# Rotated keys from a permutation of raw keys, and free-engine choice for standardisation and addends, in a planned three-layer decoder kernel

## The chip, the cores and the metric

The kernel runs on one core of a Trainium2 chip. A core has five engines with queues of their own: TensorE (PE, matmuls and transposes; PEld is its loading of the stationary operand), VectorE (DVE), ScalarE (ACT), GpSimd (POOL), and SyncE (SP), which here issues all DMAs. The metric is the device time of one execution in microseconds, and the times given are medians over several runs of the same program.

## The reference, cut to what matters

Two sequences (batches) of 512 tokens with 1024 features pass through three layers, each with a residual: an attention with 32 heads and 8 key heads and sign weights; a "state" layer; and a dense layer with low-rank additions. In float32 throughout. The change lies in the state layer's attention (16 heads of 16), in normalisations, and in how softmax maxima are handed to the scores.

```python
def rope(x, pos):                       # half = 8
    ang = pos[..., None] * inv
    cos, sin = jnp.cos(ang)[:, :, None, :], jnp.sin(ang)[:, :, None, :]
    x1, x2 = x[..., :half], x[..., half:]
    return jnp.concatenate([x1 * cos - x2 * sin, x2 * cos + x1 * sin], axis=-1)
...
qkv_in = rat_read(layernorm(x), read_w, read_g, read_b, 3)   # grouped read, then normalised to 256 x 3
q, k, v = (y @ w.T for y, w in zip(split(qkv_in, 3), qkv_w))
q, k = rope(q, pos), rope(k, pos)
p = softmax(where(causal, q @ k.T / sqrt(16), -1e30))
o = p @ v
```

After it come a write of `o` back into the state (`rat_write`), a second read of two parts, a gated unit over 1024 context columns, and a second write.

## The kernel before

The whole program is one sequence of named steps, written as Python generators (`build`, L1656 on). Each `yield` names an engine, a cost in us and the time at which its inputs are ready. A small planner (`run`) takes at each turn the step that can start first, plus its lag, and emits its instructions; the lags of jobs stand in `build`, those of spawned sub-jobs in the table `LAGS`. What the planner emits is pinned in that order, so the order on each engine is fixed when the program is built. On the chip each engine runs its own queue in order and waits on semaphores, whatever costs the planner assumed.

Buffers come from pools with fixed counts: 2 PSUM `bank`s (128x512 f32), 3 PSUM `pair`s (two banks each), and `slab`, `probs`, `page`, `row` tiles in SBUF. A step that needs a buffer takes one that an earlier step has given back.

The jobs, for batches 0 and 1:

- `in0`, `in1`, `k`, `v`, `q`, `wo`, `proj0`, `proj1`: inputs split into three bf16 parts, sign weights, projections of the first attention.
- `maxA`, `maxB` (`peaks_1`): row maxima of the scores of the first attention, 8 groups of 4 heads per batch. TensorE makes scores into two pairs, DVE reduces each pair (`reduced`). When a group of four query tiles is done, `turned` splits the negated maxima (128x16) into three bf16 addends in `parts` with four DVE operations; TensorE transposes them into a bank (`maxB_bank`), and ACT copies them to a `shift` tile.
- `attA`, `attB` (`attend`): scores again, transposed, plus a matmul of a 3x128 block of `ones16` with `shift`, which adds the negated maximum; ACT takes the exponentials; DVE adds them up; TensorE multiplies them with the values.
- `outA`, `outB`: output projection, with clean-up on DVE and POOL; rows are stored to `kept`.
- `rot`, `tableA`, `tableB`: sines and cosines and their layout into a table of 3 x 512 columns: for queries, for keys, for keys with halves exchanged.
- `stateW`, `stateA`, `stateB` (`state_inputs`): load a row, statistics, standardise 128x1024 on DVE, then `read`: transposes, a grouped matmul, statistics of three parts of 256, standardise each on DVE, transpose back with gains. Then projections: three weights `proj[0..2]` with four groups each. Each group takes two matmuls of 128x512 in f32 into a bank. Queries (kind 0) are multiplied by their table into `qq`; keys (kind 1) into `kk`; kind 2 is the key weight with the halves of each head exchanged, multiplied by the third table into a row and added to `kk` (`rotated`).
- `maxC`, `attC`, `maxD`, `attD`: the same two passes as above for the state attention, causal, four groups each. maxC works on stateA's result, maxD on stateB's.
- `tailW`, `tailA`, `tailB` (`tail`): write, second `read` with two parts of 256, gated unit, second write.
- `factor`, `factorsB`, `weights`, `denseA`, `denseB`: low-rank factors and the dense layer.

The third key weight and its use, as they stand before:

```python
for kind in range(3):
    t = yield from self.fetch(self.proj[kind], a["proj"][:, kind], 512)
...
for kind, (y, dst) in enumerate(((ys[0], qq), (ys[1], kk), (ys[1], None))):
    w = self.proj[kind]
```

In the profile all vector, scalar and GpSimd operations of the planned part have line L51 (a recording helper), all matmuls L130 and all transposes L133, so the tiles' names tell them apart: job, kind of buffer.

## Time and profile before

| what | us |
|---|---|
| median of 3 runs (1135.48 to 1136.71) | 1136.23 |
| the profiled execution | 1135.51 |
| its span on the core | 1133.8 |
| mean granted TensorE clock in it | 0.965 of full speed |

The profile's page gives for each engine its busy time, and a granted clock of TensorE in tenths per slice; a chain of waits that ended last, followed back from the last instruction; and groups of instructions by tile. A window view gives the busy time of every engine between two times. A view on one tile gives the instructions that write or read it, with the least, median and greatest duration in ns.

Where TensorE waited longest for another engine, in total, one instruction's waits together:

| TensorE instruction waits for | us | times | longest |
|---|---|---|---|
| transposes of the first input, for DVE | 8.7 | 1 | 8.7 |
| maxD scores, for DVE's maxima (buffers) | 3.9 | 5 | 2.2 |
| maxB transposes, for the addends on DVE | 3.4 | 1 | 3.4 |
| first dense transposes, for DVE | 3.2 | 2 | 2.8 |
| maxB scores, for DVE's maxima (buffers) | 3.1 | 7 | 0.9 |

### The profile page before, as it was taken

To read this page: it belongs to the slowest core of one execution; us is meant where nothing else is said; L and a number is where in the kernel's file an instruction comes from. 1 tells how busy PE (TensorE), PEld (TensorE's weight loads), DVE (VectorE), ACT (ScalarE), POOL (GpSimd) and SP (SyncE) were. 2 spreads that over 40 slices of the span, in tenths; PEclk is the share of its full clock that TensorE was granted. 3 is DMA by queue.
4 is the path that set the end of the run, shared out by engine and by line. 5 is a ranking of instruction groups with operands and counts; after the bars stand their busy time and mean duration, and the time that the engine had idled before them with its cause. 6 is when DMAs were issued, how large, how long until landed. Compare 5 with 4: busy or idle time off the path is not lost.

```text
span 1133.8 us, 16121 instructions
## 1 busy us (share of the span) xinstructions
PE 1063.1 (94%) x6364; PEld 521.5 (46%) x6364; DVE 841.2 (74%) x1390; ACT 442.8 (39%) x711; POOL 239.2 (21%) x249
## 2 busy tenths in 40 slices
PE   4889999999999998999999899989988899999998
PEld 3554353333233632332555543545465465665643
DVE  7978888578878865887777961599668677788572
ACT  6762101388500215786221255224743232332310
POOL 3442333322222303454451012001200000000000
PEclk9999999999998997999999889979998999999999
DMA  6621000101214221240113000410151001011110
GB/s 256 203 82 28 20 10 20 29 20 29 61 33 177 95 64 39 61 168 1 38 56 116 8 11 16 172 38 1 57 197 68 33 20 55 11 48 38 38 37 38
DMA packets 24784, 70.51 MB, mean 62 GB/s; under 512 B 5234, under 2 KB 5252, under 8 KB 23684
## 3 DMA queue, kind: packets, MB, share of 16 engines
q1 hardware_dynamic: 24708, 69.48, 17.9%
q8 instruction: 50, 0.82, 0.3%
q14 instruction: 26, 0.21, 0.1%
HBM read 50.59 MB, written 10.49 MB: 54 GB/s over the span
## 4 chain that ended last, share of the span: by engine, by line
PE 79%; DVE 11%; ACT 5%; issue 2%; DMA 1%; POOL 1%; SPq 0%; ACTq 0%; DVEq 0%; POOLq 0%
PE proj_bank L130 8%; PE denseA_pair L130 6%; PE denseB_pair L130 6%; PE attA_pair L130 4%; PE outA_bank L130 4%; PE attB_pair L130 4%; PE tailB_bank L130 3%; PE attB_bank L130 3%; PE attA_bank L130 3%; PE maxB_pair L130 3%; PE maxA_pair L130 3%; PE tailA_bank L130 3%; PE outB_bank L130 3%; PE stateB_bank L130 3%; PE tailB_pair L130 3%; PE tailA_pair L130 3%
## 5 line engine op out<-in xcount | busy, mean ns | idle before, releaser
L51 DVE TENSOR_REDUCE maxB_mx<-maxB_pair 128x2 f32<-128x1024 f32 x64 | 75.3, 1217 | 21.7 <-PE maxB_pair L130 21.3
L51 DVE TENSOR_REDUCE maxA_mx<-maxA_pair 128x2 f32<-128x1024 f32 x64 | 75.5, 1216 | 14.0 <-PE maxA_pair L130 14.0
L130 PEld LDWEIGHTS <-start_slab 128*128 128x128 bf16 x480 | 44.7, 98 | 68.8 <-issue 21.1
L51 DVE TENSOR_TENSOR attB_probs<-attB_probs,attB_probs 128x1024 f32<-128x1024 f32 x46 | 62.6, 1401 | 13.8 <-PE attB_bank L130 13.5
L51 ACT ACTIVATE attB_probs<-attB_pair 128x1024 f32<-128x1024 f32 x64 | 62.6, 1023 | 20.9 <-PE attB_pair L130 10.8
L51 DVE TENSOR_TENSOR attA_probs<-attA_probs,attA_probs 128x1024 f32<-128x1024 f32 x46 | 56.6, 1282 | 16.9 <-PE attA_bank L130 8.5
L51 ACT ACTIVATE attA_probs<-attA_pair 128x1024 f32<-128x1024 f32 x64 | 62.1, 1021 | 9.7 <-PE attA_pair L130 9.4
L130 PE MATMUL proj_bank<-in_slab,start_slab 128*128 128x512 bf16 x240 | 55.5, 379 | 1.7 <-ACT in_slab L51 1.7
L130 PE MATMUL proj_bank<-in_probs,start_slab 128*128 128x512 bf16 x240 | 54.7, 380 | 0.0
L130 PE MATMUL maxB_pair<-maxB_row,proj_slab 32*128 32x512 f32 x256 | 47.4, 687 | 3.1 <-DVE maxB_mx L51 3.1
L51 POOL TENSOR_SCALAR proj_row<-proj_row 128x512 f32<-128x512 f32 x24 | 47.7, 1987 | 1.9
L130 PE MATMUL outA_bank<-wo_slab,attA_slab 128*128 128x512 bf16 x192 | 46.7, 392 | 0.7 <-ACT maxB_shift L51 0.7
L130 PE MATMUL attB_pair<-proj_slab,attB_row 32*128 32x512 f32 x256 | 46.7, 685 | 0.0
L51 ACT ACTIVATE proj_row<-proj_bank,cs 128x512 f32<-128x512 f32 x20 | 13.7, 686 | 80.8 <-PE proj_bank L130 60.2
L130 PE MATMUL outB_bank<-wo_slab,attB_slab 128*128 128x512 bf16 x192 | 43.3, 379 | 0.3 <-POOL attB_slab L51 0.3
L130 PE MATMUL attA_pair<-proj_slab,attA_row 32*128 32x512 f32 x256 | 41.6, 639 | 0.3 <-ACT attA_probs L51 0.3
L51 POOL MEMSET tailB_row<- 9x128 f32 x8 | 1.6, 195 | 186.4 <-PE tailB_bank L133 70.7
L130 PE MATMUL attB_bank<-attB_probs,proj_slab 128*32 128x512 f32 x256 | 38.4, 633 | 1.1 <-DVE tableA_slab L51 0.7
L51 ACT COPY maxB_shift<-maxB_bank 128x512 bf16<-128x512 bf16 x8 | 4.7, 586 | 84.7 <-PE maxB_bank L133 84.7
L51 POOL TENSOR_SCALAR proj_slab<-proj_row 128x512 f32<-128x512 f32 x24 | 14.9, 621 | 106.6 <-ACT proj_row L51 89.0
L130 PE MATMUL maxA_pair<-maxA_row,proj_slab 32*128 32x512 f32 x256 | 36.8, 640 | 0.0
L51 POOL TENSOR_SCALAR_AFFINE_SELECT attD_probs<-attD_probs 128x512 f32<-128x512 f32 x16 | 12.1, 754 | 113.8 <-ACT attD_probs L51 104.3
(410 smaller groups left out, 2321.8 us busy)
## 6 DMA issues: line engine op xcount, KB each, us to landing
in_page<-in_x_dram SPq DMA_DIRECT2D x8, 512.0 KB, 4.1
q_page<-in_q_weight_dram SPq DMA_DIRECT2D x8, 512.0 KB, 5.3
wo_page<-in_o_weight_dram SPq DMA_DIRECT2D x8, 512.0 KB, 3.4
tailW_slab<-in_write_dram SPq DMA_DIRECT2D x3, 752.0 KB, 7.1
maxA_row<-proj_slab SPq DMA_DIRECT2D x32, 64.0 KB, 2.0
attA_row<-proj_slab SPq DMA_DIRECT2D x32, 64.0 KB, 2.0
maxB_row<-proj_slab SPq DMA_DIRECT2D x32, 64.0 KB, 2.0
outA_page<-in_x_dram SPq DMA_DIRECT2D x4, 512.0 KB, 3.7
```

The source lines that it names most:

```text
L51: return self.kernel.pin(getattr(self.engine, name)(*args, **kw))
L130: self.pin(self.nc.tensor.matmul(*args, **kw))
```

## The change

Five things are changed.

1. The third key weight is gone from the inputs, from the loads and from the projections. Keys are projected once into a bank. ACT copies the raw keys to a row, DVE multiplies the bank by the second table into `kk`, TensorE multiplies a constant 128x128 matrix `swap` (the identity with the halves of every 16 rows exchanged) with the raw row into a second bank, and DVE multiplies that by the third table and adds it to `kk`. Keys now come before queries.
2. The addends are split from the maxima instead of the negated maxima, and the constant that multiplies them is -1 instead of 1. The four operations go to DVE or POOL, whichever is free first by the planner's clock (costs 0.9 and 1.2).
3. The standardisations of `state_inputs` and `read` go through a new step `standard`, which takes DVE, or, when DVE is busier than ACT, computes an offset on POOL and applies scale and offset on ACT.
4. The pairs of norm factors kept for the tail are made on POOL.
5. Lags, start conditions and `SPARE` are new, so the order on every engine differs from the first addends of maxA (97 us in the profile before) on.

```diff
+        self.swap = self.const([P, P], "swap")
+        halves = [t.rearrange("p (e h i) -> p e h i", h=2, i=8) for t in (self.swap, self.ident)]
+        for h in range(2):
+            nc.vector.tensor_copy(halves[0][:, :, h, :], halves[1][:, :, 1 - h, :])
...
-    SPARE = 3
+    SPARE = 2.5
...
-        t = yield "DVE", 1.2, t
+        by, cost = min(("DVE", 0.9), ("POOL", 1.2), key=lambda e: self.free[e[0]] + e[1])
+        t = yield by, cost, t
+        e = nc.vector if by == "DVE" else nc.gpsimd
...
-        nc.vector.tensor_scalar(parts[:, :, :, 0], mx, -1.0, None, ALU.mult)
-        nc.vector.scalar_tensor_tensor(rest, mx, -1.0, parts[:, :, :, 0], ALU.mult, ALU.subtract)
-        nc.vector.tensor_copy(parts[:, :, :, 1], rest)
-        nc.vector.tensor_tensor(parts[:, :, :, 2], rest, parts[:, :, :, 1], ALU.subtract)
+        e.tensor_copy(parts[:, :, :, 0], mx)
+        e.tensor_tensor(rest, mx, parts[:, :, :, 0], ALU.subtract)
+        e.tensor_copy(parts[:, :, :, 1], rest)
+        e.tensor_tensor(parts[:, :, :, 2], rest, parts[:, :, :, 1], ALU.subtract)
...
-                    s[j // 2][:, j % 2, q0:], lhsT=self.ones16[r, :], rhs=shift[r, q0:], start=False, stop=True
+                    s[j // 2][:, j % 2, q0:], lhsT=self.minus16[r, :], rhs=shift[r, q0:], start=False, stop=True
...
+    def standard(self, parts, n, t):
+        nc = self.io
+        if self.free["DVE"] <= max(self.free["ACT"], t) + 0.5:
+            t = yield "DVE", (0.15 + n / 1500) * len(parts), t
+            for x, mean, r in parts:
+                nc.vector.tensor_scalar(x, x, mean, r, ALU.subtract, ALU.mult)
+        else:
+            t = yield "POOL", 0.2 * len(parts), t
+            off = self.small([P, 3], "off")
+            for i, (x, mean, r) in enumerate(parts):
+                nc.gpsimd.tensor_scalar(off[:, i : i + 1], mean, r, -1.0, ALU.mult, ALU.mult)
+            t = yield "ACT", (0.2 + n / 1310) * len(parts), t
+            for i, (x, mean, r) in enumerate(parts):
+                nc.scalar.activation(x, x, AF.Identity, scale=r, bias=off[:, i : i + 1])
+        return t
...
-            t = yield "DVE", 1.3, t
-            nc.vector.tensor_scalar(x, x, mv[:, 0, 0:1], r, ALU.subtract, ALU.mult)
             keep = self.small([P, 2], "norm", bufs=8)
-            nc.vector.tensor_copy(keep[:, 1:2], r)
-            nc.vector.tensor_scalar(keep[:, 0:1], mv[:, 0, 0:1], r, -1.0, ALU.mult, ALU.mult)
+            yield "POOL", 0.4, t
+            nc.gpsimd.tensor_copy(keep[:, 1:2], r)
+            nc.gpsimd.tensor_scalar(keep[:, 0:1], mv[:, 0, 0:1], r, -1.0, ALU.mult, ALU.mult)
+            t = yield from self.standard([(x, mv[:, 0, 0:1], r)], D, t)
...
+        def keyed(bank, g, t):
+            tr = max(t, (yield from self.take("row")))
+            tr = yield "ACT", 0.59, tr
+            raw = self.row([P, S])
+            nc.scalar.copy(raw, bank)
+            t = yield "DVE", 0.69, t
+            nc.vector.tensor_tensor(kk[:, g, :], bank, table[:, 1, :], ALU.mult)
+            self.give("bank", max(t, tr))
+            room = yield from self.take("bank")
+            tr = yield "PE", 0.97, max(tr, room)
+            other = self.bank([P, S])
+            self.mm(other, lhsT=self.swap, rhs=raw, start=True, stop=True)
+            t = yield "DVE", 1.38, max(t, tr)
+            nc.vector.tensor_tensor(raw, other, table[:, 2, :], ALU.mult)
+            self.give("bank", t)
+            nc.vector.tensor_tensor(kk[:, g, :], kk[:, g, :], raw, ALU.add)
+            self.give("row", t)
+            return t
...
-        for kind, (y, dst) in enumerate(((ys[0], qq), (ys[1], kk), (ys[1], None))):
-            w = self.proj[kind]
+        for kind, y in ((1, ys[1]), (0, ys[0])):
...
-                ("attB", self.attend_1(1, "maxB"), -1.0, "maxB"),
+                ("attB", self.attend_1(1, "maxB"), 0.2, "maxB.3"),
...
-                ("maxC", self.peaks_2(0, "stateA"), 0.5, "stateA"),
+                ("maxC", self.peaks_2(0, "stateA"), 0.2, "stateA"),
...
-                ("attC", self.attend_2(0, "maxC"), 0.2, "maxC.0"),
-                ("factorsB", self.factors_back(), 0.2, "attD"),
-                ("maxD", self.peaks_2(1, "stateB"), 0.5, "stateB", "attC.scores"),
-                ("tailW", self.tail_weights(), -0.5, "attC", "stateB"),
+                ("attC", self.attend_2(0, "maxC"), 0.0, "maxC"),
+                ("factorsB", self.factors_back(), 20.0, "attC"),
+                ("maxD", self.peaks_2(1, "stateB"), 0.5, "stateB", "maxC"),
+                ("tailW", self.tail_weights(), 3.0, "attC", "stateB"),
...
-                ("attD", self.attend_2(1, "maxD"), 0.2, "maxD.1"),
+                ("attD", self.attend_2(1, "maxD"), 0.2, "maxD"),
```

## The prediction

> **What bounds the kernel now.** I read the busy totals first, then the chain of waits, then the windows of the stretches where TensorE loses time, and last the instructions on the tiles that the change touches.
>
> ```profile
> PE 1063.1 (94%) x6364; PEld 521.5 (46%) x6364; DVE 841.2 (74%) x1390; ACT 442.8 (39%) x711; POOL 239.2 (21%) x249
> ...
> PEclk9999999999998997999999889979998999999999
> ...
> PE 79%; DVE 11%; ACT 5%; issue 2%; DMA 1%; POOL 1%; SPq 0%; ACTq 0%; DVEq 0%; POOLq 0%
> ```
>
> TensorE is busy 94% of 1133.8 us and is 79% of the chain that ended last, so matmuls removed inside a busy stretch should shorten the run one for one. DVE is 11% of that chain: in a few places TensorE waits for it. The clock row has dips in those places. Summed over windows of 5 us, TensorE is idle for 70.9 us and loses another 39.9 us of full-speed time to a granted clock under 1. Idle time of 21 us lies before 80 us, where loads start, and 5 us at the last store; neither is touched.
>
> The windows of five stretches (start:end, length, then PE, PEld, DVE, ACT, POOL busy with their counts, granted clock, DMA share, GB/s):
>
> ```profile
> 303.00:431.00 128.00, 120.83 (x572) 50.69 (x575) 102.92 (x151) 13.06 (x22) 29.19 (x32) 0.94 0.26 88
> 605.00:673.00 68.00, 62.69 (x429) 36.12 (x427) 56.64 (x130) 22.47 (x54) 1.92 (x3) 0.87 0.10 34
> 735.00:765.00 30.00, 24.92 (x164) 13.67 (x162) 27.78 (x53) 6.88 (x15) 0.00 (x0) 0.77 0.10 36
> 850.00:890.00 40.00, 33.41 (x154) 18.97 (x153) 30.18 (x60) 13.68 (x28) 0.20 (x1) 0.83 0.20 75
> 591.00:606.00 15.00, 14.55 (x37) 6.31 (x35) 10.22 (x16) 1.16 (x3) 6.24 (x5) 1.00 0.31 105
> ```
>
> The maxima of batch 1's first attention (303 to 431), the state layer's maxima maxC (605 to 673) and maxD (735 to 765) have DVE busy 80 to 93% and the low clocks. The projections of the state layer (591 to 606) have TensorE at 14.55 of 15 us and clock 1.00: there TensorE alone is the bound.
>
> **The keys' permutation.** The rows of the projection's matmuls and evictions:
>
> ```profile
> L130 PE MATMUL stateA_bank<-stateA_probs,stateW_slab x48: 592/592/697, 591.5 to 613.8; 128*128 128x512 f32 x48
> L51 DVE TENSOR_TENSOR stateA_slab<-stateA_bank,tableA_slab x8: 636/690/692, 593.4 to 606.5; 128x512 f32<-128x512 f32 x8
> L51 DVE TENSOR_TENSOR stateA_row<-stateA_bank,tableA_slab x4: 637/680/692, 608.1 to 614.6; 128x512 f32<-128x512 f32 x4
> ```
>
> The trace records each f32 matmul twice: 24 in the code, 48 here. They overlap, so the price is not 592 ns: by windows on this tile those 48 fill 20.91 us, 0.436 us each. The third weight's 8 matmuls per batch go (16 records), 4 with the swap matrix come (8 records). Net 16 records over both batches, 16 x 0.436 = 7.0 us less, on an engine that is full. **-7.0.** DVE does the same three operations per key group, 0.69 us each. ACT gains 8 copies of 128x512 out of PSUM, bounded by the ACT copy of the same form at 0.59 us: 4.7 us on an engine that is 39% busy, in a stretch where it had 1.16 us of work in 15. One load of 512 KB goes; DMA is at 31% there and nothing waits for it.
>
> The new wait is projection, ACT copy, swap matmul. The built order has k0, k1, swap0, swap1: k1 (4 records, 1.74 us) covers the first copy (0.59). Behind a late swap stand on TensorE the next projection, and on DVE two operations of its group. In batch 1 these steps run among attC's exponentials, 1.03 and 0.81 us each on ACT; a copy behind two of them is 1.8 us late. Bounds: 0, or 4 x 1.8 = 7.2; attC's own matmuls stand between, so I take the low side, **+1.5**.
>
> **The addends.** Batch 1's rows; all 24 groups have the same form:
>
> ```profile
> L51 DVE TENSOR_SCALAR parts<-maxB_mx x8: 201/202/203, 312.4 to 429.3; 128x16 bf16<-128x16 f32 x8
> L51 DVE SCALAR_TENSOR_TENSOR maxB_rest<-maxB_mx,parts x8: 183/184/185, 312.6 to 429.5; 128x16 f32<-128x16 f32 x8
> L51 DVE CAST parts<-maxB_rest x8: 201/202/203, 312.9 to 429.8; 128x16 bf16<-128x16 f32 x8
> L51 DVE TENSOR_TENSOR parts<-maxB_rest,parts x8: 228/230/231, 313.1 to 430.0; 128x16 bf16<-128x16 f32 x8
> ```
>
> Four operations make 0.82 us. In the built program 19 of 24 groups stand on POOL (4 of maxA, 7 of maxB, all of maxC and maxD), so DVE loses 19 x 0.82 = 15.6 us. The minus sign moves into a constant matrix of -1 and costs nothing on any engine: one memset replaces another. Of standardisations, all 4 rows of 1024 in stateA, 2 rows of 1024 and 6 of 256 in stateB, 4 of 256 in each tail leave DVE for ACT (0.81 and 0.40 us on DVE); the eight pairs of norm factors (0.15 + 0.20) go to POOL. ACT pays 6 x 1.23 (its row on tailA_slab, 128x1024) and 14 x 0.37 (copy of 128x256): 12.6 us. The eight tail rows, 3.2 us, sit after 765 where TensorE has other work; I count them at nothing, and if that cover were gone they would be worth 3.2 at most. The two copies that build the swap matrix fall in DVE's 2.85 us wait for the first input; if uncovered they cost 0.8 by the neighbouring copy of 0.41.
>
> Where does freed DVE time count? In maxA TensorE is full from 100 to 200: nothing, and nothing to lose unless POOL is late. In 605 to 673 DVE loses 4 x 0.82 + 4 x 0.35 + 2 x 0.81 + 6 x 0.40 = 8.7 us. TensorE loses 5.3 idle and 8.8 to the clock there. Bounds: a loss of 2.8, since attC now waits for the whole of maxC and no longer for its first group (it began at 661.7 and the last addends ended at 664.5), and a gain of 8.7; **-4.4**, half the gain, as the new order keeps matmuls of stateB's reading between the maxima. In 735 to 765 DVE loses 3.3, against 5.1 idle and 6.9 clock; bounds 0 and 10.2 (the 3.3 with the whole dip); **-3**, as DVE stays at about 24 of 30.
>
> **POOL in DVE's place** has no row for 128x16. Bounds: four memsets of 128x1 at 0.10, 0.4 us; four copies of 128x128 at the slowest tile:
>
> ```profile
> L51 POOL COPY tableA_row<-rotations x12: 291/298/301, 438.1 to 440.7; 128x128 f32<-128x128 f32 x12
> L51 POOL COPY tableB_row<-rotations x12: 292/1014/1289, 478.3 to 492.3; 128x128 f32<-128x128 f32 x12
> ```
>
> that is 4 x 1.01 = 4.1 us; the plan allows 1.2. Sixteen elements are nearer the small end; I take four of 0.25, inside the plan. The same copy costs 0.30 while DVE reads nothing and 1.01 while DVE adds probabilities, so the neighbour matters. What waits for late addends is a transpose on TensorE, with everything behind it. **+1.**
>
> The Trainium skill's GPSIMD Engine Reference, "Specifications", says POOL shares its SBUF interfaces with VectorE and contends with two-input or two-port DVE work. That speaks against handing POOL work just when DVE is busy, and agrees with the two copy rows; but a maximum out of PSUM is neither kind. By it the price would stay at 1 us a group in the maxima and rise by about three only beside two-input work.
>
> **The start of attB.** The windows there:
>
> ```profile
> 426.00:427.00 1.00, 0.87 (x6) 0.04 (x3) 0.90 (x2) 0.00 (x0) 0.51 (x1) 1.00 0.00 0
> 427.00:428.00 1.00, 0.00 (x0) 0.00 (x0) 1.00 (x1) 0.00 (x0) 0.00 (x0) 1.00 0.00 0
> 428.00:429.00 1.00, 0.00 (x0) 0.00 (x0) 1.00 (x2) 0.00 (x0) 0.00 (x0) 1.00 0.00 0
> 429.00:430.00 1.00, 0.00 (x0) 0.00 (x0) 0.86 (x5) 0.00 (x0) 0.00 (x0) 0.64 0.00 0
> 430.00:431.00 1.00, 0.72 (x8) 0.53 (x11) 1.00 (x3) 0.07 (x1) 0.00 (x0) 0.50 0.00 0
> ```
>
> TensorE waits 3.4 us for four maxima and the last addends; the clock halves at 429.6 and stays 0.50 until 442.5, which costs 12.9 / 2 = 6.5 us more. In the new order outA's matmuls are spread to the end of maxB, and attB's first 8 matmuls and their shifts (about 2 us) stand ahead of the last transposes. But those need PSUM pairs that the same maxima free, so I reckon 2.6 us of idle in pieces instead of 3.4 in one. Bounds 0 (the same maxima end the wait in both orders, so a loss is excluded) and 9.9; I take a third, **-3**.
>
> The Trainium skill's "TensorE: Matmul & The Clock Gate", Part 1, has the clock back after about 3.4 us of activity. The trace shows 12 us after the first matmul at 430.3. By the page the dip would be worth some 2 us, by the row 6.5.
>
> **Moved steps and the sum.** outA, factors, tables, tail and dense steps keep their instructions but change places; the loads factorsB and tailW move on SP's queue, which nothing waits for here. From 850 on, 6.6 idle and 6.8 clock could be won or as much lost; 0. Sum: -7.0 + 1.5 - 4.4 - 3 + 1 - 3 = -14.9. The profiled execution took 1135.5 (span 1133.8 and 1.7 around it), so 1120.6; its time is 0.7 under the median of 1136.2, which gives **1121 us**.
>
> **Rivals.** Only the matmuls count: the stalls move but stay, 1136.2 - 7 = 1129. For it: DVE stays the second limit in all maxima. Against: 12 us of its work leave just those stretches. All dips close: -7 - 9.9 - 8.7 - 10.2 = 1100. Against: DVE keeps 24 of 30 us in maxD. The slower case is late addends: a POOL group takes the upper 4.1 us, 2.9 over the plan's 1.2, in front of 19 groups of transposes in TensorE's fixed order; full exposure 55 us gives 1176, and from 15 / 19 = 0.8 us exposed per group it is slower than before. For it: POOL's 1.01 row; against: sixteen elements, and outA matmuls that stand between most groups of maxB and their transposes. That the new places in the dense part lose what the front wins, 1136, is the case of no change: 15 us of new stall in a part that now loses 13.
>
> **Chances.** Forecast 0.48 (1113 to 1127), matmuls alone 0.25, all dips 0.12, late addends 0.10, dense part 0.05. Two runs of this kernel can be told apart by about 0.2%. Faster 0.85, same 0.04, slower 0.11. Range 1105 to 1137: it takes in both nearer rivals' bounds, and leaves out the far ends.
>
> **What would show it.** 32 projection records per batch and 8 of the swap, about 17.4 us instead of 20.9 in stateA; addend operations on POOL of 0.1 to 0.3 us; clock over 0.9 in maxC and maxD; TensorE's first wait for attB under 3 us. A TensorE wait named after POOL's addends, longer than 0.8 us and repeated, or after the copy stateB_row, would prove me wrong.

## The result and the profile after

The changed kernel is slower. Its median is 1141.78 us (1138.99 to 1147.28 in 7 runs), the kernel before in the same job had 1136.22 (1131.48 to 1136.71 in 7 runs): 1.0061 times, 95% interval [1.0038, 1.0085]. The slowdown is small, 0.6%, but the interval excludes an equal time. The profiled execution took 1147.28 with a span of 1145.6 and a mean granted clock of 0.950, against 1135.51, 1133.8 and 0.965 before. It is the slowest of the seven, 5.5 us over their median, so what is read from its trace overstates the change by about that much.

The page of the changed kernel, its busy totals, its clock row and its chain of waits:

```profile
PE 1070.8 (93%) x6348; PEld 523.2 (46%) x6348; DVE 815.1 (71%) x1286; ACT 457.6 (40%) x733; POOL 275.5 (24%) x361
...
PEclk9999999999998998999999699868989998999999
...
PE 74%; DVE 11%; ACT 7%; DMA 3%; issue 2%; POOL 1%; SPq 1%; ACTq 0%; POOLq 0%; DVEq 0%
```

VectorE has 26 us less to do, near the 28 that the prediction's counts come to, and it is still 11% of the chain. TensorE has 16 records fewer and is busy 7.7 us longer, which goes with the lower clock: the row now has a 6 in two slices. DMA, which was 1% of the chain, is 3%.

The windows that answer to the prediction's five (start:end, length, then PE, PEld, DVE, ACT, POOL busy with their counts, granted clock, DMA share, GB/s): maxB, maxC with what lies around it, all of maxD, the dense weights, the projections.

```profile
303.00:428.50 125.50, 119.27 (x565) 49.84 (x558) 92.86 (x118) 12.79 (x21) 35.41 (x55) 0.95 0.25 86
605.00:661.00 56.00, 49.97 (x328) 31.55 (x327) 40.84 (x77) 20.85 (x48) 8.13 (x32) 0.78 0.15 57
719.00:783.00 64.00, 55.61 (x332) 33.20 (x331) 42.12 (x78) 16.51 (x30) 6.99 (x19) 0.76 0.13 50
847.00:890.00 43.00, 39.98 (x199) 24.11 (x198) 31.05 (x56) 13.10 (x27) 1.33 (x4) 0.88 0.18 62
588.00:606.00 18.00, 16.86 (x39) 6.72 (x38) 13.65 (x23) 3.41 (x7) 6.24 (x5) 1.00 0.26 88
```

For the second and third, the kernel before from the first matmul of maxC to that of attC, and from the first of maxD to that of attD:

```profile
622.10:661.70 39.60, 36.20 (x287) 22.86 (x286) 37.18 (x83) 11.41 (x30) 0.00 (x0) 0.87 0.08 28
724.20:771.20 47.00, 41.44 (x266) 22.28 (x265) 39.26 (x83) 13.27 (x25) 0.00 (x0) 0.85 0.06 23
```

VectorE is busy 73% and 66% now, where it was 94% and 84%, and the clock is 0.78 and 0.76 for 0.87 and 0.85. VectorE had more room and TensorE did not go faster.

For a balance I cut both spans at the first matmul of each stage, and summed in windows of 2 us what TensorE stood idle and what it lost to a clock under 1 (length times one minus the clock). What is left of a stage's length is, roughly, work at full clock.

| stage | before: length (idle, clock) | after: length (idle, clock) | change of idle + clock |
|---|---|---|---|
| all up to maxB's end | 430.8 (29.8, 9.3) | 428.5 (29.0, 8.6) | -1.5 |
| attB, outB | 160.7 (4.1, 6.1) | 159.4 (4.7, 3.4) | -2.1 |
| stateA's projections | 30.6 (1.8, 0) | 25.9 (1.4, 0) | -0.4 |
| maxC | 39.6 (3.4, 5.1) | 47.5 (5.8, 12.6) | +9.9 |
| attC | 62.5 (1.6, 3.4) | 57.7 (1.3, 1.0) | -2.7 |
| maxD | 47.0 (5.6, 6.8) | 64.1 (8.4, 15.3) | +11.3 |
| attD | 72.9 (4.3, 0) | 64.0 (6.0, 3.4) | +5.1 |
| dense weights, dense | 289.7 (20.2, 9.2) | 298.5 (18.2, 12.4) | +1.2 |

Idle and clock rise by 20.8 us and the span by 11.8, so TensorE's work fell by 9.0. At the first matmul of maxC the changed kernel is 8.3 us ahead (613.8 against 622.1); at the first of attC 0.4 us; at the first of attD it is 11.9 behind.

The largest single wait that the kernel before did not have is in maxD. The timeline of the changed kernel, TensorE (start, length, engine, line, operation, out<-in, count, and in brackets the idle time before it and what ended it):

```profile
719.69 2.75 PE L130 MATMUL tailA_bank<-tailW_slab,attC_slab 128*128 128x376 f32 x8
...
723.01 0.40 PE L130 MATMUL maxD_pair<-late,ident 128*128 128x128 bf16 x4
728.17 0.36 PE L133 MATMUL tailA_bank<-ident,tailA_few 128*8 128x128 f32 x1 [4.76 <-ACT tailA_row L51]
```

The same view for ACT:

```profile
718.27 0.37 ACT L51 COPY stateB_slab<-stateB_bank 128x256 f32<-128x256 f32 x1 [1.54 <-PE stateB_bank L130]
724.07 3.80 ACT L51 ACTIVATE tailA_slab<-tailA_slab,stateA_norm 128x1024 f32<-128x1024 f32 x3 [5.43 <-DMA tailA_slab<-kept]
727.77 0.35 ACT L51 COPY tailA_row<-tailA_bank 128x256 f32<-128x256 f32 x1
```

And SP's queue, where the loads are issued:

```profile
614.33 2.60 SPq L142 DMA_DIRECT2D factorsB_slab<-factor  x2
705.33 0.33 SPq L142 DMA_DIRECT2D tailW_slab<-in_write_dram  x1
...
707.53 0.85 SPq L142 DMA_DIRECT2D tailW_probs<-in_ctx_dram  x2
708.43 1.64 SPq L142 DMA_DIRECT2D tailW_slab<-in_write_dram  x2
...
715.48 1.31 SPq L142 DMA_DIRECT2D tailA_slab<-kept  x3
```

Read from the end. TensorE's next transpose goes into the bank that ACT's copy reads, and waits for that copy. The copy had its input when the matmuls into the bank ended, at 722.4 by the same view, but three activations stand ahead of it in ACT's order, and those wait for three rows of 512 KB, which land at 724. The rows were issued at 715.48, behind 2 MB of context and 2.25 MB of write weights. In the kernel before, SP's queue has one write slab much earlier and the factors much later:

```profile
619.72 0.43 SPq L142 DMA_DIRECT2D tailW_slab<-in_write_dram  x1
...
711.63 1.42 SPq L142 DMA_DIRECT2D tailA_slab<-kept  x3
...
837.06 0.97 SPq L142 DMA_DIRECT2D factorsB_slab<-factor  x2
```

There ACT ran its three activations from 724.55 on with no wait for DMA. In the new order the factors take the two slabs that come free at 614, and the first write slab has to wait until attC is over (SP waits 88.5 us for attC's scores there). The rows themselves take no longer to land than before, 8.6 to 10.1 us after their issue for 9.9 to 11.4. What differs is that they are issued 3.9 us later and that ACT comes to them 5.9 us earlier, at 718.64: the issue is 3.2 us ahead of ACT, where it was 12.9.

### The profile page after: what moved, and what is told of

It reads as the page before. It is cut to its first block, busy times and chain, and to the rows that moved or that the text cites. A ratio compares the mean times of both kernels' runs of the same rounds, so it can differ in the third digit from the quotient of the medians.

```text
span 1145.6 us, 16104 instructions
## 1 busy us (share of the span) xinstructions
PE 1070.8 (93%) x6348; PEld 523.2 (46%) x6348; DVE 815.1 (71%) x1286; ACT 457.6 (40%) x733; POOL 275.5 (24%) x361
## 4 chain that ended last, share of the span: by engine, by line
PE 74%; DVE 11%; ACT 7%; DMA 3%; issue 2%; POOL 1%; SPq 1%; ACTq 0%; POOLq 0%; DVEq 0%
PE proj_bank L130 8%; PE denseB_pair L130 5%; PE denseA_pair L130 5%; PE attA_pair L130 4%; PE tailA_bank L130 4%; PE attB_bank L130 4%; PE attA_bank L130 4%; PE outA_bank L130 4%; PE attB_pair L130 3%; PE maxA_pair L130 3%; PE tailB_bank L130 3%; PE maxB_pair L130 3%; PE factor_bank L130 3%; PE tailB_pair L130 3%; PE outB_bank L130 2%; PE stateB_bank L130 2%
## 5 line engine op out<-in xcount | busy, mean ns | idle before, releaser
L51 DVE TENSOR_REDUCE maxA_mx<-maxA_pair 128x2 f32<-128x1024 f32 x64 | 75.4, 1218 | 17.6 <-PE maxA_pair L130 17.6
L51 DVE TENSOR_TENSOR attB_probs<-attB_probs,attB_probs 128x1024 f32<-128x1024 f32 x46 | 61.3, 1370 | 15.4 <-ACT attB_probs L51 8.2
L51 ACT ACTIVATE attB_probs<-attB_pair 128x1024 f32<-128x1024 f32 x64 | 62.5, 1024 | 22.8 <-PE attB_pair L130 15.4
L130 PE MATMUL outA_bank<-wo_slab,attA_slab 128*128 128x512 bf16 x192 | 47.7, 397 | 0.6 <-DVE outA_row L51 0.6
L130 PE MATMUL maxB_pair<-maxB_row,proj_slab 32*128 32x512 f32 x256 | 42.8, 648 | 1.6 <-DVE maxB_mx L51 1.6
L51 ACT ACTIVATE proj_row<-proj_bank,cs 128x512 f32<-128x512 f32 x20 | 13.7, 686 | 75.9 <-PE proj_bank L130 75.9
L130 PE MATMUL attB_pair<-proj_slab,attB_row 32*128 32x512 f32 x256 | 41.7, 658 | 0.2 <-DVE maxB_mx L51 0.2
L130 PE MATMUL attB_bank<-attB_probs,proj_slab 128*32 128x512 f32 x256 | 41.2, 619 | 0.3
L130 PE MATMUL attA_bank<-attA_probs,proj_slab 128*32 128x512 f32 x256 | 34.1, 605 | 0.0
L130 PEld LDWEIGHTS <-attA_slab 128*128 128x128 bf16 x192 | 18.0, 101 | 33.9 <-issue 15.7
```

Of the source, the lines that this page charges most:

```text
L51: return self.kernel.pin(getattr(self.engine, name)(*args, **kw))
L130: self.pin(self.nc.tensor.matmul(*args, **kw))
```

## The experiments

Ratios are to the kernel before, run beside each on the same chip.

**Once more, and plan against code.** The changed kernel unaltered; its code with the old lags, start conditions and `SPARE`; the old code with the new ones; and the old code and plan with the permutation alone (keys first, as in the change), all planned by the kernel's own planner.

```diff
 newcode_oldplan: the changed file with
-    LAGS = {... "maxC.turned": -0.6, ...}   SPARE = 2.5   ("attC", ..., 0.0, "maxC"), ...
+    LAGS = {... "stateA.rotated": -0.1, ...}   SPARE = 3   ("attC", ..., 0.2, "maxC.0"), ...
 oldcode_newplan: the file before with the same lines the other way round
 swap_only: the file before with
+        self.swap ...
-        for kind, (y, dst) in enumerate(((ys[0], qq), (ys[1], kk), (ys[1], None))):
+        for kind, y in ((1, ys[1]), (0, ys[0])):
```

> The changed kernel once more, unaltered, for a second trace: its profiled execution took 1147.3 us while the median of its runs was 1141.8. Every theory expects 1139 to 1144. The theory that a free-running clock window makes the runs differ expects the granted clock of this trace to go with its time: above 0.953 if it is faster than 1141, and the low-clock places to be partly others than in the first trace.

> All code of the change (swap, addends, standardisation, norm factors), but lags, start conditions and SPARE of before, so the planner makes a third order. Theory P (the new plan loses what the operations win): 1121 to 1132, faster than before by 4 us or more. Theory O (the operations themselves cost the time, by taking DVE's work off and leaving TensorE's low clock): 1136 to 1146 again.

> The code of before under the new lags, start conditions and SPARE. Theory P: slower than before by 6 us or more, 1142 to 1155, with the loss in maxC and between maxD and attD. Theory O: within 4 us of before, 1132 to 1140.

> Before, with the keys' permutation alone (third weight gone, keys before queries), under the old plan. By the sum of the prediction 16 records of 0.436 us less on TensorE: 1129 to 1131 if the later order stays as good. If a later stretch gives it back, stateA's projections are still 3.5 us shorter than 29.9 and the total is 1133 to 1139.

| run | median us | ratio, 95% interval |
|---|---|---|
| after_again | 1145.57 | 1.0084 [1.0058, 1.0110] |
| newcode_oldplan | 1158.06 | 1.0203 [1.0183, 1.0224] |
| oldcode_newplan | 1180.92 | 1.0416 [1.0378, 1.0455] |
| swap_only | 1156.40 | 1.0191 [1.0172, 1.0210] |

The median of after_again is above the 1139 to 1144 that every theory expected. Its trace, again the slowest of its runs, repeats the first stage by stage (maxC 47.4 us with 5.8 idle and 12.6 clock, maxD 64.0 with 8.4 and 15.4). The three mixtures are all worse than both kernels. A different set of steps or values gives a different order, and each of these three orders, planned by values meant for other code, costs 20 us or more. swap_only shows it best: its projections are 4.8 us shorter, and it loses 13 us from the first dense matmul on, where it changes no operation. All three times lie outside every range on record for them. Runs that let the planner work again cannot price an operation. From here on the order was kept: the planner sees the old steps and only the emitted instructions differ.

**One operation in the old order.**

```diff
 swap_fixed
-                self.accumulate(bank, [(w[:, i, g * P : (g + 1) * P], y[:, i, :]) for i in range(2)])
+                if kind == 2: self.mm(bank, lhsT=self.swap, rhs=raw[g], start=True, stop=True)
+                else: self.accumulate(...)
...
+            if kind == 1: nc.scalar.copy(raw[g], bank)
 before_pool_addends
+        e = nc.gpsimd
-        nc.vector.tensor_scalar(parts[:, :, :, 0], mx, -1.0, None, ALU.mult)
+        e.tensor_copy(parts[:, :, :, 0], mx)
...
```

> The kernel before, instruction for instruction in its own order, with one thing changed: where the third weight was multiplied (16 matmul records per batch in two matmuls for each of four groups) there stands one matmul with the permutation on a copy of the raw keys, and ACT makes that copy where the first product is emitted. No step of the plan moves. Theory F (the operations of the change are worth what their rows say, and what the new order costs is something else): about 1136 - 7 = 1129, stateA's projections near 26 instead of 30.6 us, ratio 0.992 to 0.996, no TensorE wait after the copy over 1 us. Theory S (the saving is used up at once where the next stage is held by VectorE): stateA's projections shorter by the same 4 to 5 us and maxC longer by as much, total 1134 to 1138, ratio 0.998 to 1.002. If the copies hold up ACT, slower than 1138 with waits named after the raw copies.

> The kernel before in its own order, with the four short operations of every addend group emitted on POOL instead of VectorE (all 24 groups), nothing else. Theory F: POOL's operations take 0.25 us each as in the changed kernel, VectorE loses some 1.2 us of work a group in the maxima, so 2 to 5 us less in maxB, maxC and maxD together: 1131 to 1135. Theory L (late addends): the four take up to 4 us a group beside VectorE's reductions, TensorE waits for them in front of the transposes by over 0.8 us in most groups, and the time goes over 1140. Theory S: the maxima are not set by VectorE's work but by the clock, 1135 to 1138.

swap_fixed: 1138.77, 1.0032 [1.0012, 1.0052]. The saving is hardly there, even in the stage itself. Its timeline of TensorE shows why:

```profile
606.93 1.02 PE L130 MATMUL stateA_bank<-stateA_slab,swap 128*128 128x512 f32 x2
608.77 1.12 PE L130 MATMUL stateA_bank<-stateW_slab,swap 128*128 128x512 f32 x2 [0.82 <-DVE stateA_slab L51]
610.50 1.10 PE L130 MATMUL stateA_bank<-stateW_slab,swap 128*128 128x512 f32 x2 [0.60 <-DVE stateA_row L51]
...
613.06 1.13 PE L130 MATMUL stateA_bank<-stateW_slab,swap 128*128 128x512 f32 x2 [0.67 <-ACT stateB_page L51]
```

By windows on this tile the projections' matmuls fill 18.4 us instead of 21.3, 2.9 less, but the stretch from the first to the last shrinks only from 22.9 to 21.7 us, and the stage from 30.6 to 30.0. Two banks go round, and each third product needs two operations of 0.69 us on VectorE, among which stand the statistics and the standardisation of two rows of stateB. VectorE has hardly a gap from 606.6 to 617.3: it is busy 10.45 of 10.70 us. The third weight's matmuls were covered by that; the shorter ones uncover it. The theory that the rows' price is paid out (1129) falls, and the other has the place wrong: the saving is used up by VectorE in the stage itself, before maxC (40.6 us for 39.6). The time lies above both theories' ranges, in the range of the third, held-up copies; but the waits of the swap matmuls are not named after the raw copies, they are named after VectorE's products and ACT's stateB_page.

before_pool_addends: 1139.60, 1.0064 [1.0042, 1.0086], slower. The waits of TensorE for the addends in the whole run (total, times, longest):

```profile
PE maxB_bank L133 <- POOL parts L51: 4.4, 1, 4.4
...
PE maxA_bank L133 <- POOL parts L51: 2.6, 3, 1.6
...
PE maxC_bank L133 <- POOL parts L51: 2.1, 1, 2.1
...
PE maxD_bank L133 <- POOL parts L51: 1.6, 1, 1.6
```

In the kernel before, VectorE's addends make TensorE wait 3.4 us in maxB, 1.3 in maxC, 0.7 in maxD and not at all in maxA. POOL's are about 1 us later where nothing covers them, which in maxA is the last group above all (1.56 us at 209.7); maxA grows from 132.9 to 135.9 us. The change puts only the first 4 of maxA's 8 groups on POOL and has no such wait there. Against these stand attB and attC, each 1.9 us shorter. The theory of late addends is right in direction and nearly in the total (1139.6 for over 1140), and wrong in size: it is the last groups of the stages, not most groups.

**One operation taken back in the new order.**

```diff
 after_dve_addends
-        e = nc.vector if by == "DVE" else nc.gpsimd
+        e = nc.vector
 after_dve_standard: in `standard`, second branch
...
-                nc.scalar.activation(x, x, AF.Identity, scale=r, bias=off[:, i : i + 1])
+                nc.vector.tensor_scalar(x, x, mean, r, ALU.subtract, ALU.mult)
 after_third
-            nc.scalar.copy(raw, bank)
...
-            self.mm(other, lhsT=self.swap, rhs=raw, start=True, stop=True)
+            self.accumulate(other, [(w[:, i, g * P : (g + 1) * P], ys[1][:, i, :]) for i in range(2)])
```

> The changed kernel in its own order, with the addends of all 24 groups emitted on VectorE (in the new three-operation form) instead of 19 of them on POOL; nothing else differs. If POOL's part relieves VectorE as the prediction reckoned (1.2 us a group in maxB, maxC and maxD), this is 3 to 9 us slower than the changed kernel: ratio to the kernel before 1.010 to 1.016. If the place does not matter, because VectorE and POOL end such a wait equally late, the same within 2 us: 1.006 to 1.009. If POOL's addends are late, faster: under 1.005.

> The changed kernel in its own order, with the standardisations that it put on POOL and ACT (stateA, stateB, tailA, tailB) emitted on VectorE as in the kernel before, at the same places. If they relieve VectorE where it sets the pace, slower by 2 to 8 us than the changed kernel: ratio 1.009 to 1.015. If they hold ACT's queue, and so the PSUM banks that ACT empties for stateB's reading, they cause the low clock of maxC: then maxC falls from 47.5 to under 44 us and the ratio is under 1.005. If neither, 1.006 to 1.009.

> The changed kernel in its own order, with the third weight loaded again and its 16 matmul records per batch in place of the permutation and the copy of the raw keys. In the kernel before, the permutation alone brought nothing, since VectorE's products held the shorter matmuls. Theory K (keys first makes the saving real: queries' matmuls cover the products of the keys): stateA's projections go back from 25.9 to 29 to 31 us and the time rises by 4 to 8 us over the changed kernel, ratio 1.010 to 1.016. Theory S (the saving is lost again in the stages behind): the projections grow, maxC shrinks by as much, ratio 1.006 to 1.009.

| run | median us | ratio, 95% interval |
|---|---|---|
| after_dve_addends | 1145.63 | 1.0095 [1.0066, 1.0124] |
| after_dve_standard | 1144.06 | 1.0081 [1.0057, 1.0106] |
| after_third | 1143.95 | 1.0078 [1.0057, 1.0099] |

The changed kernel itself had 1.0061 and 1.0084. From the mean of these, 1.0073, the three differ by 0.0022, 0.0008 and 0.0005: 2.5 us at most, inside the intervals. Each operation can be taken out by itself without a change that four runs can tell. The bounds are loose: the upper ends of the intervals leave some 6, 4 and 3 us for them, and after_dve_addends lies between the two ranges of its expectation, so a small relief by POOL is not excluded. after_third is the clearest: with the third weight back the projections take 27.5 us instead of 25.9 and maxC 43.6 instead of 47.5, attC 59.9 instead of 57.7. What keys-first saves in the projections is waited for again in the stages behind, as that expectation's second theory had it.

**The loads.**

```diff
 after_ctx_late: tail_weights and tail, SP's queue alone
-            t = yield from self.fetch(self.ctx[h], a["ctx"][:, 2 * h : 2 * h + 2], 1024)
+            t = yield "SP", 0.06, 0.0
...
         th = yield from self.fetch(xs, self.kept[b][q][:, :], 512)
+        # behind the third of these
+            for h in range(2): self.load(self.ctx[h], self.a["ctx"][:, 2 * h : 2 * h + 2])
```

> The changed kernel in its own order on every compute engine; on SP's queue alone the two loads of the context (1 MB each), which stand ahead of the first three rows of tailA's state (0.5 MB each), are issued behind them. In the changed kernel ACT waits 5.4 us for these rows, and TensorE 4.8 us for a copy that stands behind them on ACT. Theory Q (the order of the loads made this stall, and the low clock of maxD follows from it): the rows arrive 4 to 6 us earlier, the 4.8 us wait goes to under 1 us, maxD and attD together fall by 5 to 12 us from 128, and the time to 1131 to 1138. Theory V: the wait goes but maxD's clock stays low and attD starts as late, so that the time falls by 0 to 3 us, to 1139 to 1142. If the context is then late for tailA's own matmuls, a wait for it shows and the time does not fall.

1136.41 us, 1.0018 [0.9999, 1.0037]: by the ratios 5 us under the changed kernel's first measurement and 7.5 under its repetition. Its timeline of ACT and then of TensorE at the same place:

```profile
714.26 2.51 ACT L51 ACTIVATE tailA_slab<-tailA_slab,stateA_norm 128x1024 f32<-128x1024 f32 x2 [0.44 <-DMA tailA_slab<-kept]
717.36 1.24 ACT L51 ACTIVATE tailA_slab<-tailA_slab,stateA_norm 128x1024 f32<-128x1024 f32 x1 [0.59 <-DMA tailA_slab<-kept]
718.51 0.35 ACT L51 COPY tailA_row<-tailA_bank 128x256 f32<-128x256 f32 x1
```

```profile
718.20 0.40 PE L130 MATMUL maxD_pair<-late,ident 128*128 128x128 bf16 x4
718.91 0.27 PE L133 MATMUL tailA_bank<-ident,tailA_few 128*8 128x128 f32 x1 [0.32 <-ACT tailA_row L51]
```

The rows land 4.5 to 5.7 us after their issue instead of 8.6 to 10.1, the wait of 4.76 us is 0.32, and maxD takes 57.9 us instead of 64.1 (4.0 idle, 13.7 clock). The stall goes when the rows are not queued behind the context: shown. The context stands ahead of the rows in the kernel before too, so the run does not say how much of the stall came from the later write slab and how much from ACT's earlier arrival. That the low clock follows from the stall is not shown: 13.7 us of it stay. attD stays at 64.1, so the two together fall by 6.1 us, the low end of the first theory. With this the changed kernel is level with the one before: the late rows are as much as it was slower by, and what remains to be explained is the 15 us that it was to gain.

**The clock.** In the changed kernel two long stretches run at half clock, by the window view:

```profile
626.00:643.00 17.00, 16.62 (x84) 8.36 (x83) 11.54 (x23) 3.61 (x8) 1.73 (x7) 0.50 0.00 1
742.00:762.00 20.00, 18.77 (x96) 9.74 (x96) 17.24 (x28) 3.44 (x6) 3.25 (x8) 0.50 0.15 54
```

TensorE is busy 98 and 94% there, mostly with scores of 32 rows, and VectorE, which set the pace in the kernel before, now waits for it. The total waits of VectorE for maxC's scores, first before, then after (us, times, longest):

```profile
DVE maxC_mx L51 <- PE maxC_pair L130: 1.4, 3, 0.9
```

```profile
DVE maxC_mx L51 <- PE maxC_pair L130: 11.0, 8, 2.8
```

Two runs added matmuls that add zero to the scores, to keep the clock up: after_fill behind the scores of query tiles 2 and 3, after_ctx_keep ahead of the transposes at which the clock had fallen, on top of the late context.

```diff
 after_fill, in peaks, ahead of the masks
+                    for jj in range(2 if nk > 256 else 0):
+                        self.mm(s[1][:, jj, :nk]..., lhsT=self.ident16, rhs=nil..., start=False, stop=False)
 after_ctx_keep
+                    for i in range(8 if g and qt == 1 else 0):
+                        self.mm(s[1][:, i % 2, :nk]..., lhsT=self.ident16, rhs=nil..., start=False, stop=False)
```

> The changed kernel in its own order, with extra matmuls in the two causal maxima maxC and maxD: for query tiles 2 and 3 of each group two bf16 matmuls of 128 rows by 384 or 512 columns that add zero to the scores, about 0.2 us each at full clock, 6 to 7 us of added TensorE work in all. Theory C (in maxC and maxD of the changed kernel TensorE is held at half clock because the scores use a quarter of its rows at a time and no full-array work stands between them): the clock in these two stretches rises from 0.73 and 0.76 to over 0.9 and the time falls by 5 to 18 us in spite of the added work, to 1124 to 1137. Theory V (these stretches are held by VectorE's maxima and by late buffers; the low clock is only their consequence): the clock stays under 0.85 there and the time rises by 2 to 7 us, to 1144 to 1149.

> The changed kernel with the context loaded late (1136.4 us) and, in the causal maxima, eight matmuls that add zero (bf16, 128 rows by 256 columns, some 0.9 us at full clock) put just ahead of the transposes of groups 0 to 2, that is into the place where TensorE stood 0.30 and 0.83 us before the clock fell to half for 17 us in maxC. 6 groups, 5 to 6 us of added work in all. Theory C (the clock falls because of these short waits and then stays low because only 32-row scores follow): maxC's clock loss goes from 12 to under 5 us, maxD's from 14 to under 8, and the time falls to 1122 to 1133. Theory V (VectorE's reductions set these stretches whatever the clock): clock loss may fall, but the lengths of maxC and maxD stay within 2 us or grow, 1136 to 1142.

after_fill: 1144.57, 1.0107 [1.0079, 1.0136]; in its trace maxC takes 49.2 us at clock 0.79 and maxD 63.0 at 0.89, so neither theory's clock came in both stages, and the time is that of the second. after_ctx_keep: 1138.44, 1.0022 [1.0002, 1.0043], the same as without the added matmuls. Its windows of maxC and maxD, under those of after_ctx_late:

```profile
610.20:657.50 47.30, 41.31 (x289) 25.24 (x288) 34.61 (x65) 17.90 (x39) 6.79 (x28) 0.75 0.15 57
714.20:772.10 57.90, 53.89 (x334) 32.72 (x333) 41.87 (x78) 16.49 (x30) 6.79 (x19) 0.76 0.17 67
```

```profile
611.50:658.10 46.60, 40.46 (x313) 26.63 (x312) 34.53 (x65) 17.68 (x39) 6.79 (x28) 0.85 0.15 57
714.80:774.30 59.50, 51.82 (x360) 32.77 (x359) 42.27 (x80) 16.30 (x30) 7.02 (x19) 0.89 0.17 65
```

The clock rose from 0.75 and 0.76 to 0.85 and 0.89, which takes 12.0 us off its loss by the 2 us windows. Work at full clock grew by 9.1 us (the expectation had 5 to 6) and idle time by 3.8; the lengths stayed within 2 us, as the second theory had it. So more full-array work does bring the clock back here, but no time comes of it. Whether the low clock costs time that could be had more cheaply is not settled by these two runs: in maxC the filler itself may have eaten the gain, while in maxD the idle time grew, which speaks for VectorE and the buffers. after_third points the other way for maxC: there, with no filler, the clock's loss is 6.8 us instead of 12.6 and maxC lasts 43.6 us instead of 47.5. So a low clock as a cause of maxC's length is not excluded.

**The order in maxC, and the parts together in the old order.**

```diff
 after_old_c
-                ("maxC", self.peaks_2(0, "stateA"), 0.2, "stateA"),   ("attC", ..., 0.0, "maxC"),   "maxC.turned": -0.6
+                ("maxC", self.peaks_2(0, "stateA"), 0.5, "stateA"),   ("attC", ..., 0.2, "maxC.0"),
 before_pool_bcd: before_pool_addends with
-        e = nc.gpsimd
+        e = nc.vector if name == "maxA" else nc.gpsimd
 before_swap_std: swap_fixed with, in state_inputs,
...
-            nc.vector.tensor_scalar(x, x, mv[:, 0, 0:1], r, ALU.subtract, ALU.mult)
+            nc.scalar.activation(x, x, AF.Identity, scale=keep[:, 1:2], bias=keep[:, 0:1])
 before_swap_std_bcd: both
```

> The changed kernel, planned with the old values for maxC and attC alone (their lags, attC allowed to begin with maxC's first group, no advance for the addends' transposes); the order up to stateA stays, all behind it is planned anew. In the changed kernel maxC and attC take 105.2 us together, before 102.1, and with the change's operations under the whole old plan 95.2. Theory R (the values of these two stages put the work in an order that loses 10 us there): 94 to 98 us here. Theory V (the two are held by VectorE and the PSUM buffers in any order, and the 95.2 came from work left to later stages): 102 to 106. The total is no test, since maxD and all behind it are planned anew: 1135 to 1165.

> The kernel before in its own order, with the addends on POOL in maxB, maxC and maxD and left on VectorE in maxA. With all 24 groups on POOL, maxA grew by 3.0 us and attB and attC shrank by 1.9 each. Theory F (the relief is real, the loss was maxA's): 2 to 4 us less than before, ratio 0.996 to 0.999. If the shorter attB and attC were the run's own spread: 1.000 to 1.004.

> The kernel before in its own order with the permutation on the copied keys and, besides, the standardisation of stateA's and stateB's rows on ACT and its two small norm operations on POOL. In the permutation alone TensorE waited for VectorE's products in the last eight matmuls of stateA, among which VectorE standardised two rows of stateB (1.2 us each). Theory K (the saving is real as far as VectorE is relieved at the same place): the projections of stateA fall from 30.0 to 27 or 28 us, and the time to 1131 to 1136. Theory S: shorter projections, longer maxC, 1136 to 1140.

> The two edits of the runs beside it together, in the order of the kernel before: permutation, standardisations on ACT, addends on POOL but in maxA. Theory K and F: they add up, 1129 to 1134, under both kernels. If VectorE's relief brings nothing in this order: 1136 to 1141.

| run | median us | ratio, 95% interval |
|---|---|---|
| after_old_c | 1161.53 | 1.0227 [1.0205, 1.0249] |
| before_pool_bcd | 1136.97 | 1.0006 [0.9998, 1.0015] |
| before_swap_std | 1138.83 | 1.0031 [1.0018, 1.0045] |
| before_swap_std_bcd | 1138.65 | 1.0021 [1.0008, 1.0034] |

after_old_c has maxC and attC at 102.7 us (41.3 and 61.4), not 94 to 98: the planner's values of the two stages are worth at most 2.5 of the 10 us, by one trace, and the theory that they alone lose it falls. Everything behind stateA is planned anew there, so its total measures nothing more. In before_pool_bcd maxA is 132.9 again and the whole equals the kernel before: the relief of VectorE in the maxima of the old order is worth nothing that 11 runs can see, POOL's later ends included (TensorE waits 4.4 us for the last addends of maxB, for 3.4). In before_swap_std the projections take 29.4 us instead of 30.0, with outB 3.9 us longer (61.9 for 58.0): the first theory's 27 to 28 us do not come. VectorE, though relieved of the standardisations, is still busy 9.17 of the 9.38 us from 608.45 to 617.83, which agrees with swap_fixed. No version tried beats the kernel before; after_ctx_late and before_pool_bcd equal it.

## Why the prediction was wrong

The forecast was 1121 us, range 1105 to 1137, faster. The time is 1141.78: above the range, and on the other side.

- **Permutation, -7.0.** The row was read rightly: by windows on the tile the projections' matmuls of stateA fill 17.9 us instead of 21.3, 3.4 of the 3.5 per batch that the sum has (its 20.91 is of a window that ends half a microsecond early). The step that failed is the one from there to the end, "matmuls removed inside a busy stretch should shorten the run one for one". In the new order the stage did shrink, from 30.6 to 25.9 us, but with the same 16 records put back the time did not move beyond the noise (after_third); in the old order the stage itself kept its length (swap_fixed). The prediction had read VectorE's 10.22 us in the window that ends at 606. The third weight's products and sums come behind it, and there VectorE is as near to being the limit as TensorE; the kernel before:

```profile
606.00:614.60 8.60, 7.93 (x25) 3.74 (x23) 8.28 (x19) 1.58 (x5) 0.00 (x0) 1.00 0.00 0
```

- **Waits of the swap, +1.5.** About right: no wait is named after the copy, and 1.1 us after VectorE's products in stateA.
- **maxC, -4.4.** Measured +9.9, or +7.2 with attC, whose start the prediction's window takes in. The clock, which was to be over 0.9 here and in maxD, is 0.73 in maxC and 0.76 in maxD. VectorE was indeed relieved (34.6 us busy in maxC for 37.2), and no gain from the relief is seen: putting the addends or the standardisations back on VectorE in the new order changes neither maxC (47.7 and 46.9 us for 47.5) nor, within the noise, the total. "Half the gain, as the new order keeps matmuls of stateB's reading between the maxima" is what failed: in the stretch from 626 to 643 hardly any of them stand between, and the lower bound of -2.8 was drawn from attC's start alone.
- **maxD, -3, bounded by 0 and 10.2.** Measured +11.3. A loss had been excluded. Some 6 us of it are the late rows.
- **Moved steps, 0.** "The loads factorsB and tailW move on SP's queue, which nothing waits for here" is false, and the wait for the late rows is the one price that a run shows by itself: 5 to 7.5 us. attD's start belongs here too. The gate of the first tail tile moved ahead of attD's first scores, and its products on VectorE hold PSUM pairs that the second scores need. In after_ctx_late, where the loads are out of the way, the timeline of TensorE still has

```profile
773.28 0.59 PE L130 MATMUL tailA_bank<-tailW_slab,tailA_row 9*128 9x256 f32 x2
777.16 1.66 PE L130 MATMUL attD_pair<-stateB_slab,stateB_slab 32*128 32x384 f32 x8 [3.29 <-DVE tailA_page L51]
```

- **POOL's addends, +1.** Right in size, 0.25 us for most operations, with 0.5 to 0.77 for some in maxA and maxB. The slow ones bear out the prediction's point on the neighbour. Two rows of the changed kernel, for maxA and maxC, and then the timelines of POOL and of VectorE at one of the slow places:

```profile
L51 POOL CAST parts<-maxA_rest x4: 760/770/771, 100.5 to 146.4; 128x16 bf16<-128x16 f32 x4
...
L51 POOL CAST parts<-maxC_rest x4: 253/254/257, 624.2 to 660.1; 128x16 bf16<-128x16 f32 x4
```

```profile
99.94 0.50 POOL L51 TENSOR_TENSOR maxA_rest<-maxA_mx,parts 128x16 f32<-128x16 f32 x1
100.51 0.77 POOL L51 CAST parts<-maxA_rest 128x16 bf16<-128x16 f32 x1
```

```profile
99.67 0.68 DVE L51 SCALAR_TENSOR_TENSOR proj_slab<-proj_row,proj_slab 128x512 f32<-128x512 f32 x1
100.46 0.75 DVE L51 COPY_PREDICATED proj_slab<-proj_row,proj_row 128x512 f32<-128x512 int32 x1
```

Both slow operations end within 0.1 us of a VectorE operation that reads two tiles of SBUF. At 624.2, where VectorE reads a bank in PSUM, the same CAST takes 0.26.

TensorE waits for POOL's addends once, 1.7 us at the end of maxB, so the rival on the slower side, late addends, is not what happened. It is real where the cover ends (before_pool_addends).

- **attB, -3.** Right: idle and clock of attB fall by 2.0 us and maxB's by 1.7, and the first scores of attB come 2.3 us earlier. The half clock that the prediction read from 429.6 to 442.5 lasts, by windows of 0.1 us, from 429.3 to 442.9, which is 6.8 us of loss for its 6.5.
- **Dense part, 0.** Right within 1.2 us, as the sum of 2.0 us less idle time and 3.2 more of clock. The 6.6 and 6.8 us that the prediction gives for "from 850 on" are those of 850 to 890 alone; the whole part had 20.2 and 9.2.

What remains unsettled is the greater part of the new order's loss in maxC, maxD and attD, 17.6 us of idle and clock in the slowest trace, attC's gain taken off, besides the 6 of the late rows. Shown is that none of the three operations, taken out by itself, brings it back, that a second trace repeats the stages' lengths, that the values of maxC and attC carry 2.5 us of it at most, and that raising the clock by filler does not shorten it. That it lies in how stateB's reading and the tail are strewn among the maxima is the explanation left over, and it is argued, not shown. Giving the free slabs to the write weights before the factors, and moving the tail's gate behind attD's first scores, were not tried.

## What to carry to other kernels

When one change edits operations and also plans the order anew, price the order first: put each edit into the old order by itself, and each old operation back into the new one. Before counting a removed matmul, look in the very slots it leaves at what the next engine is doing; behind a stretch with TensorE at 97% the removed matmuls can stand in one where a second engine is at its limit too. Every load that moves on an in-order queue needs the list of what is ahead of it and of what its first reader stands in front of.

## What the runs showed of the hardware

A granted clock of 0.50 lasted 17 and 20 us while TensorE was busy 98 and 94% of the time, mostly in score matmuls of 32 rows. By windows of 0.1 us these stretches last 17.0 us (625.9 to 642.9) and 20.5 (741.9 to 762.3), and the one in the kernel before 13.65 (429.3 to 442.9): 5, 6 and 4 times 3.41 us. The Trainium skill's "TensorE: Matmul & The Clock Gate", Part 1, has the clock back after about 3.4 us of activity; the rows here disagree, unless matmuls that use a quarter of the array count for less. Eight bf16 matmuls of 128 rows by 256 columns in three of the four groups raised the clock of those stages from 0.75 to 0.85 and from 0.76 to 0.89.

The same operation of 16 elements per partition on POOL takes 0.25 us in maxC and 0.77 us in the first half of maxA, beside VectorE operations that read two tiles of SBUF.

Both kernels spread widely from run to run: 29 runs of the kernel before, in one job, lie between 1131.81 and 1138.19 us, the changed kernel's 14 between 1138.77 and 1149.29. One trace against one trace cannot tell differences of 3 us here.
